# First block's inverse, edges and sums dealt out among its n_h products, and the first adjacency loads kept in text order: a two-layer graph network on one core

## The chip, the cores and the metric

The kernel runs on one core of a Trainium2 chip. The metric is the device time of one execution in microseconds (us); the time of a kernel is the median of its runs. Five engines work beside each other, each through its own instructions in order: TensorE (PE, matrix products; PEld is its weight load), VectorE (DVE), ScalarE (ACT), GpSimd (POOL) and SyncE (SP), which issues most of the transfers. They wait for each other through semaphores only.

## The reference, cut to what matters

`x` is 128 x 128 x 256 (batch, nodes, channels), `adj` 128 x 128 x 128 of zeros and ones, all in float32.

```python
h = relu(layernorm(x))
# layer 0, per batch element
c  = relu(bn1(conv1x1(h.T)));  c = bn2(conv17(c))          # along the nodes
x_conv = relu(c + h.T).T
s  = h @ w_se.T + b_se                                     # 3 columns
A  = exp(-dist(s, s)) * adj
x_nmp = A @ relu(h @ w_msg.T + b_msg)
gi = concat(x_conv, x_nmp) @ w_ih.T + b_ih
gh = h @ w_hh.T + b_hh
r, z = sigmoid(gi_r + gh_r), sigmoid(gi_z + gh_z)
n  = tanh(gi_n + r * gh_n)
x  = x + (1 - z) * n + z * h
# layer 1: five groups of the first 25 nodes, relu(layernorm(x)) again as input
for g in groups:
    N  = dinv * (adj_g + I) * dinv                         # dinv = deg ** -0.5
    o  = relu(N @ relu(N @ h_g @ W1[g] + b1[g]) @ W2[g] + b2[g])
    fused[idx_g] += softmax(fusion_w)[g] * o
x = x + fused
```

## The kernel before

The 128 batch elements go in 32 blocks of four. A front part (up to some 482 us) makes the normalised input `ht` of every block and stores it, and does the 17-wide convolution in the frequency domain: weight spectra, input spectra, products per frequency (`spectral`, lines 309 to 320), whose results lie in DRAM as `yd`. Then a main loop runs over the blocks and does the rest of layer 0; layer 1 goes in four parts (40, 40, 40 and 8 elements), the first from block 10 on, in the gaps of the main loop.

For block i the main part has these steps, each a function:

- `load(i)` (lines 458 to 473) issues on SP the loads of `ht`, of the adjacency `at`, of the frequency rows `ym` and of `yr` (four pieces of 32 rows).
- `gate_inputs(i, which)` (line 615) builds sums of quarter matrices, named `t` (lines 623 to 626, four operations of 128 x 256): `which` 2 from `ht`, 0 from `xc`, 1 from `xn`. They let a 2 x 2 block product be done with seven products in place of eight. In the kernel before those of `ht` and `xc` run on POOL, those of `xn` on DVE.
- `messages(i)` (lines 523 to 567) makes the messages `msg` and the three columns of `s` in seven products (line 535), combined on DVE (545, 546, 547, 552 to 555), ACT (548 copies `m5`) and POOL (549, 550), and ends with `lr`, the factors of the distance (561 to 566).
- `conv_out(i)` (lines 505 to 520) is the inverse of the frequency step: per half of the channels four products from `ym` (512) and one from `yr` (515), DVE adds `ht` (517), ACT takes the relu (518); the result is `xc`. It is a generator that stops after each half.
- `edge_terms(i)` transposes `lr` (573) into `lt` (copy on ACT, 575); `edges(i)` multiplies them (585), takes the exponential on ACT (588) and masks with `at` on DVE (590), giving `A_s[i]`.
- `x_nmp(i)` multiplies messages and edges (600) and copies out `xn` (603 on DVE, 605 on ACT).
- `gates(i, ...)` (line 631) does the gates in units of seven products (649), with copies on ACT (652, 660), sums on DVE (654, 657, 664, 667, 670) and on POOL (662, 668). Unit `nh` (gh_n) reads `ht` alone, `r` reads `ht`, `xc`, `xn`, `nn` reads `xc`, `xn`, and `z` all three. Sigmoid (684, 701) and tanh (694) run on ACT; 688, 693, 699, 702 and 703 are DVE's steps between. After each product the unit calls `between`.
- `back(i)` adds the result to `xt` (789), stores nodes 25 to 127 (`out`, 800) and the first 25 (`xf`, 802), and prepares layer 1's input (812 to 835). `degrees` makes the degree factors in steps (735 to 759), transposes (764) and stores them (767).
- `prepare(j)` (line 841) concerns pack j of layer 1: it loads the adjacency `nt` (846) and the factors `dck` (848, broadcast from the stored degrees) of pack j + 5, and for pack j + 2 adds the identity (852) and multiplies by `dck` (853). `nt` has eight buffers, `dck` three. Layer 1's first part calls it for j = -5 to -1 as it starts.

`beside_gates(i)` chains messages, inverse, edge terms, edges and x_nmp of block i with the back of block i - 2, one step for each `next`. In the main loop `gates(i, step, ...)` lets `step` advance block i + 1 between the products of block i. Block 0 has no block before it: its own steps run ahead of the loop until `A_s[0]` exists, and the rest of them after the sixth of its seven `nh` products (`sums_ahead`).

Where a region isn't scheduled by hand (the front is), the framework's planner orders every engine's instructions itself, so that text order isn't the order of the program: an instruction can be put earlier or later on its engine than the text has it. A buffer of a pool is given to the next tile once its last reader is placed, and that tile's first writer waits for it. PSUM has eight banks, handed on in the same way. SP issues transfers in order; an issue that has to wait holds up those behind it.

Of the kernel before, what the change touches and what calls it, by code (L numbers as in the profile page):

```python
# [75 lines left out]
def gnn_kernel(ctx: ExitStack, tc: tile.TileContext, io, out0: bass.AP, out1: bass.AP):  # L76
    nc = tc.nc
    x, adjT = io["x"], io["adjT"]
    B, N, D = x.shape
    C = D // P  # L80
# [24 lines left out]
    ident = cst.tile([P, P], F32)  # L105
# [248 lines left out]
    with front as es:  # L354
# [71 lines left out]
        begin = heads_begin(hk, xk, 3, 1)  # L426
        sums = gate_weights()
        amid = {p: lambda: next(begin, None) for p in range(16, NP_, 4) if p != 20}
# [29 lines left out]
    loaded, hts = {}, {}  # L458
# [45 lines left out]
    def conv_out(i):  # L504

        ht = hts[i]
        _, ym, yr = loaded[i]
        xc = wk.tile([P, C, T], F32, tag="xc", name="xc", bufs=2)
        for o in range(C):
            ps = bank()  # L510
            for b in range(BB):
                nc.tensor.matmul(ps[:, b * N:(b + 1) * N], ym[:, b, o * P:(o + 1) * P], idm,  # L512
                                 start=b == 0, stop=False)

            nc.tensor.matmul(ps.rearrange("p (b n) -> p b n", b=BB)[:, :, OUTW:], yr[:, o * P:(o + 1) * P], idr,  # L515
                             start=False, stop=True)
            nc.vector.scalar_tensor_tensor(xc[:, o, :], ps, sc2[:, o:o + 1], ht[:, o, :], op0=ALU.mult, op1=ALU.add)
            nc.scalar.activation(xc[:, o, :], xc[:, o, :], AF.Relu, bias=sh2[:, o:o + 1])
            yield
        xcs[i] = xc  # L520

    def messages(i):

# [91 lines left out]
    def gate_inputs(i, which=(0, 1, 2)):  # L615

        tt = ts.setdefault(i, {})
        for k in which:
            d, eng = ((xcs, nc.gpsimd), (xns, nc.vector), (hts, nc.gpsimd))[k]
            d = d[i]  # L620
            t = wk.tile([P, 4, H], F32, tag=f"t{k}", name=f"t{k}", bufs=1 + k // 2)
            b11, b12, b21, b22 = quarters(d)
            eng.tensor_tensor(t[:, 0], b12, b11, op=ALU.subtract)
            eng.tensor_tensor(t[:, 1], b22, t[:, 0], op=ALU.subtract)
            eng.tensor_tensor(t[:, 2], b22, b12, op=ALU.subtract)
            eng.tensor_tensor(t[:, 3], t[:, 1], b21, op=ALU.subtract)
            tt[k] = t

    def gates(i, between, nxt, ahead=None):

        ht, xc, tt = hts.pop(i), xcs.pop(i), ts[i]
        ins = [xc, None, ht]

        def small(name):
            return wk.tile([P, H], F32, tag=name, name=name, bufs=2)

        def unit(g, pairs, dst, order, hook=None, between=between):
            got = {}  # L640
            for j in order:
                ps = bank()[:, :H]
                for n, k in enumerate(pairs):
                    a11, a12, s1, a22 = (v[:, g] for v in gate_blocks(k))
                    s2, s3, s4 = (sw[k][:, g, m] for m in range(3))
                    b11, b12, b21, b22 = quarters(ins[k])
                    t1, t2, t3, t4 = (tt[k][:, m] for m in range(4))
                    w, d = ((a11, b11), (a12, b21), (s4, b22), (a22, t4), (s1, t1), (s2, t2), (s3, t3))[j - 1]
                    nc.tensor.matmul(ps, w, d, start=n == 0, stop=n == len(pairs) - 1)  # L649
                if j == 1:  # L650
                    got["m1"] = small("m1")
                    nc.scalar.copy(got["m1"], ps)
                elif j == 2:
                    nc.vector.tensor_tensor(dst[:, 0, :H], ps, got["m1"], op=ALU.add)
                elif j == 6:
                    got["u2"] = small("u2")
                    nc.vector.tensor_tensor(got["u2"], ps, got["m1"], op=ALU.add)
                elif j == 5:
                    got["m5"] = small("m5")
                    nc.scalar.copy(got["m5"], ps)  # L660
                    got["u4"] = small("u4")
                    nc.gpsimd.tensor_tensor(got["u4"], got["u2"], got["m5"], op=ALU.add)  # L662
                elif j == 3:
                    nc.vector.tensor_tensor(dst[:, 0, H:], ps, got["u4"], op=ALU.add)  # L664
                elif j == 7:
                    got["u3"] = small("u3")
                    nc.vector.tensor_tensor(got["u3"], ps, got["u2"], op=ALU.add)  # L667
                    nc.gpsimd.tensor_tensor(dst[:, 1, H:], got["u3"], got["m5"], op=ALU.add)
                else:
                    nc.vector.tensor_tensor(dst[:, 1, :H], got["u3"], ps, op=ALU.subtract)  # L670
                    if hook:
                        hook()
                between()

        o = wk.tile([P, C, T], F32, tag="o", name="o", bufs=2)
        r = o
        nh = wk.tile([P, C, T], F32, tag="z", name="nh", bufs=1)
        if ahead:

            unit(2, (2,), nh, (1, 2, 6, 5, 3, 7, 4), between=ahead)  # L680
        ins[1] = xns.pop(i)
        unit(0, (2, 0, 1), r, (1, 2, 6, 5, 3, 7, 4))
        for q in range(C):
            nc.scalar.activation(r[:, q, :], r[:, q, :], AF.Sigmoid, bias=brz[:, q:q + 1])
        if not ahead:
            unit(2, (2,), nh, (1, 2, 6, 5, 3, 7, 4))
        for q in range(C):
            nc.vector.scalar_tensor_tensor(r[:, q, :], nh[:, q, :], vec[:, V_HH + 4 + q:V_HH + 5 + q], r[:, q, :],
                                           op0=ALU.add, op1=ALU.mult)
        nn = wk.tile([P, C, T], F32, tag="nn", name="nn", bufs=1)  # L690
        unit(2, (0, 1), nn, (1, 2, 6, 5, 3, 7, 4))
        for q in range(C):
            nc.vector.tensor_add(nn[:, q, :], nn[:, q, :], r[:, q, :])  # L693
            nc.scalar.activation(nn[:, q, :], nn[:, q, :], AF.Tanh, bias=vec[:, V_IH + 4 + q:V_IH + 5 + q])  # L694
        z = wk.tile([P, C, T], F32, tag="z", name="z", bufs=1)
        unit(1, (2, 0, 1), z, (1, 6, 5, 7, 4, 2, 3), nxt)

        for q in range(C):
            nc.vector.tensor_sub(o[:, q, :], ht[:, q, :], nn[:, q, :])
        for q in range(C):  # L700
            nc.scalar.activation(z[:, q, :], z[:, q, :], AF.Sigmoid, bias=brz[:, 2 + q:3 + q])
            nc.vector.tensor_mul(o[:, q, :], o[:, q, :], z[:, q, :])
            nc.vector.tensor_add(o[:, q, :], o[:, q, :], nn[:, q, :])
        outs[i] = o
# [135 lines left out]
    def prepare(j):  # L840

        if 0 <= j + 5 < NPK:
            s, nb = GROUPS[PACKS[j + 5][1][0]][0], PACKS[j + 5][1][2]
            n = nb * s
            nt = l1.tile([P, P], F32, tag="nt", name="nt", bufs=8)
            nc.sync.dma_start(nt[:n, :n], io["adjN"][j + 5, :n, :n])
            dc = l1.tile([P, P], F32, tag="dck", name="dck", bufs=3)
            nc.sync.dma_start(dc[:n, :n], dvk[j + 5, :n].partition_broadcast(n))
            loads1[j + 5] = n, nt, dc
        if 0 <= j + 2 < NPK:  # L850
            n, nt, dc = loads1.pop(j + 2)
            nc.vector.tensor_add(nt[:n, :n], nt[:n, :n], ident[:n, :n])
            nc.vector.tensor_mul(nt[:n, :n], nt[:n, :n], dc[:n, :n])
            ready[j + 2] = nt

# [135 lines left out]
    def beside_gates(i):  # L991

        ends = back(i - 2, *back_loads(i - 2)) if i > 1 else iter(())
        if i < NBLK:
            parts = messages(i)
            next(parts)
            yield
            next(parts)
            next(ends, None)
            yield  # L1000
            inverse = conv_out(i)
            next(inverse)
            next(ends, None)
            yield
            edge_terms(i)
            next(ends, None)
            yield
            for _ in inverse:
                yield
            edges(i)  # L1010
            yield
            next(ends, None)
            yield
            yield
            yield from x_nmp(i)
        for _ in ends:
            yield
            if i == NBLK:
                yield
# [3 lines left out]
    degs = degrees(*degree_loads())  # L1023
    gate_inputs(0, (2,))
    begin = beside_gates(0)
    while 0 not in A_s:
        next(begin)
    gate_inputs(0, (0,))
    gate_inputs(1, (2,))
    held = [6]  # L1030

    def sums_ahead():

        held[0] -= 1
        if held[0] == 0:
            for _ in begin:
                pass
            gate_inputs(0, (1,))

    layer1s = []  # L1040
    for i in range(NBLK):
# [168 lines left out]
```

## Time and profile before

| | us |
|---|---|
| median of 4 runs | 1910.31 |
| the four runs | 1908.65, 1913.48, 1911.97, 1908.22 |
| the profiled execution | 1908.65 |
| its span, first to last instruction | 1906.8 |
| PE busy in the span | 1878.6 (99%) |
| DVE, ACT, POOL busy | 1343.0, 723.9, 667.4 |
| stage 500 to 520: PE, DVE busy | 18.97, 19.29 |
| stage 540 to 560: PE busy, mean granted clock | 16.96, 0.91 |
| stage 580 to 600: PE busy, mean granted clock | 19.96, 1.00 |

The page gives the busy time and the share of the span for each engine. A stage row (start:end) has the length of the stage, then busy time and instruction count of PE, PEld, DVE, ACT and POOL, then the clock granted to PE, the share of the DMA engines in use and GB/s. A timeline row has start, duration, engine, line, operation, what it writes and reads, shape and count; in brackets stands how long the engine was idle before it and what released it. A row of SPq is the issue of a transfer, not the transfer.

### The profile page before, as it was taken

How to read it: one execution, taken by the hardware profiler on the slowest of the kernel's cores; microseconds unless marked ns; L12 is line 12 of the kernel's file. 1: busy time of each engine (PE TensorE's matmuls, PEld its weight loads, DVE VectorE, ACT ScalarE, POOL GpSimd, SP SyncE). 2: the span in 40 equal slices, each digit the busy share in tenths (PEclk: the TensorE clock that was granted, in tenths of full speed). 3: DMA queues.
4: the chain of work that ended last, by engine and by line, in shares of the span. 5: the costliest groups of instructions: out<-in, count | busy, mean ns of one | idle time of the engine just before them, and what ended most of it. 6: DMA issues, size and time to landing. Idle time of an engine off the chain costs nothing.

```text
span 1906.8 us, 31441 instructions
## 1 busy us (share of the span) xinstructions
PE 1878.6 (99%) x10994; PEld 1643.4 (86%) x10994; DVE 1343.0 (70%) x3246; ACT 723.9 (38%) x1588; POOL 667.4 (35%) x747
## 2 busy tenths in 40 slices
PE   9999999999999999999999999999999999999998
PEld 7888889988788888888888888888888888888887
DVE  6674558754778787887666777878666688787643
ACT  5552124411333433343343343343343434334334
POOL 1113531265335445444312244544322244444200
PEclk9999999999999999999999999999999999999999
DMA  9976896289832332233244433233334434222135
GB/s 354 331 293 209 304 321 211 100 285 308 243 89 73 92 92 74 73 98 97 73 106 96 131 90 84 73 90 105 83 89 93 142 75 107 66 79 69 36 92 152
DMA packets 248877, 265.87 MB, mean 139 GB/s; under 512 B 106866, under 2 KB 223943, under 8 KB 244239
## 3 DMA queue, kind: packets, MB, share of 16 engines
q1 hardware_dynamic: 238751, 199.82, 37.5%
q10 hardware_dynamic: 9968, 64.04, 8.6%
q8 instruction: 88, 1.44, 0.3%
q14 instruction: 70, 0.57, 0.1%
HBM read 178.66 MB, written 85.14 MB: 138 GB/s over the span
## 4 chain that ended last, share of the span: by engine, by line
PE 91%; DMA 3%; DVE 3%; POOL 1%; issue 1%; ACT 0%; SPq 0%; POOLq 0%; DVEq 0%; ACTq 0%
PE bank L649 45%; PE bank L319 6%; PE bank L974 5%; PE bank L914 5%; PE bank L535 5%; PE bank L228 5%; PE bank L243 3%; PE bank L314 3%; PE bank L600 3%; PE bank L512 3%; PE bank L167 2%; DMA v<-vd 2%; PE bank L515 1%; PE bank L893 1%; PE bank L214 1%; PE bank L825 1%
## 5 line engine op out<-in xcount | busy, mean ns | idle before, releaser
L649 PE MATMUL bank<-t,sw 128*128 128x256 f32 x1152 | 291.3, 380 | 0.0
L662 POOL TENSOR_TENSOR u<-u,m 128x256 f32<-128x256 f32 x128 | 95.0, 742 | 485.3 <-ACT m L660 432.9
L649 PEld LDWEIGHTS bank<-t,sw 128*128 128x128 f32 x1152 | 215.4, 190 | 29.8 <-issue 2.3
L649 PE MATMUL bank<-t,wih 128*128 128x256 f32 x768 | 197.2, 379 | 0.0
L649 PEld LDWEIGHTS bank<-t,wih 128*128 128x128 f32 x768 | 143.4, 190 | 19.3 <-issue 0.5
L311 POOL TENSOR_TENSOR vs<-v 128x512 f32<-128x512 f32 x78 | 101.1, 1315 | 116.3 <-DMA v<-vd 67.1
L228 PE MATMUL bank<-wc,ht 128*128 128x256 f32 x512 | 118.9, 385 | 1.4 <-ACT ht L215 1.4
L649 PE MATMUL bank<-xc,wih 128*128 128x256 f32 x384 | 116.9, 386 | 0.7 <-DVE nh L664 0.2
L649 PE MATMUL bank<-t,whh 128*128 128x256 f32 x384 | 115.0, 381 | 2.3 <-DVE u L667 2.3
L558 ACT ACTIVATE msg<-msg 128x512 f32<-128x512 f32 x64 | 36.8, 621 | 210.7 <-DVE msg L554 210.7
L974 PE MATMUL bank<-w,hh 128*125 128x256 f32 (+9 forms) x480 | 113.8, 380 | 1.7 <-DVE hh L919 1.7
L649 PE MATMUL bank<-xn,wih 128*128 128x256 f32 x384 | 114.2, 379 | 0.0
L649 PE MATMUL bank<-ht,whh 128*128 128x256 f32 x384 | 110.0, 380 | 0.0
L228 PEld LDWEIGHTS bank<-wc,ht 128*128 128x128 f32 x512 | 96.3, 192 | 15.5 <-ACT ht L215 2.9
L914 PE MATMUL bank<-ax,w 128*128 128x500 f32 (+8 forms) x416 | 107.0, 396 | 0.3 <-DMA w<-in_w_dram 0.3
L309 DVE SCALAR_TENSOR_TENSOR s<-X 128x256 f32<-128x256 f32 x78 | 49.1, 632 | 82.0 <-PE bank L319 81.4
L198 POOL TENSOR_TENSOR rs<-ve,mhalf 128x4 f32<-128x4 f32 x32 | 32.8, 1026 | 205.0 <-DVE ve L196 205.0
L974 PEld LDWEIGHTS bank<-w,hh 128*125 128x125 f32 (+9 forms) x480 | 84.2, 177 | 20.3 <-DVE hh L919 2.6
L694 ACT ACTIVATE nn<-nn,vec 128x512 f32<-128x512 f32 x64 | 46.2, 722 | 135.8 <-DVE nn L693 135.8
L316 ACT COPY k<-bank 128x256 f32<-128x256 f32 x78 | 29.0, 373 | 175.6 <-DVE ys L320 70.7
L667 DVE TENSOR_TENSOR u<-bank,u 128x256 f32<-128x256 f32 x128 | 53.4, 417 | 57.7 <-PE bank L649 57.6
L314 PE MATMUL bank<-vs,X 128*128 128x256 f32 x312 | 81.6, 383 | 6.1 <-POOL vs L311 6.1
(207 smaller groups left out, 4519.8 us busy)
## 6 DMA issues: line engine op xcount, KB each, us to landing
v<-vd SPq DMA_DIRECT2D x80, 512.0 KB
vd<-sp ACTq DMA_DIRECT2D x8, 2560.0 KB
yd<-ys ACTq DMA_DIRECT2D x40, 512.0 KB
w<-in_w_dram SPq DMA_DIRECT2D x40, 512.0 KB
ln<-in_x_dram SPq DMA_DIRECT2D x32, 512.0 KB
htd<-ht ACTq DMA_DIRECT2D x32, 512.0 KB
ht<-htd SPq DMA_DIRECT2D x32, 512.0 KB
ym<-yd SPq DMA_DIRECT2D x32, 512.0 KB
```

Of the source, the lines that this page charges most:

```text
L228: nc.tensor.matmul(pv[:, bb, :], ht[:, c, b * N:(b + 1) * N], wc1[:, c, :], start=c == 0, stop=c == C - 1)
L243: nc.tensor.matmul(ps[:, bb * 2 * LW:(bb + 1) * 2 * LW], h1[:, 2 * h + bb, c * P:(c + 1) * P], fd, start=True, stop=True)
L311: nc.gpsimd.tensor_tensor(vs, vr, vi, op=ALU.add)
L314: nc.tensor.matmul(p1[:, :D], a[:, c], vs[:, c], start=c == 0, stop=c == C - 1)
L319: nc.tensor.matmul(ps[:, k * D:(k + 1) * D], u[:, c], w[:, c], start=c == 0, stop=c == C - 1)
L512: nc.tensor.matmul(ps[:, b * N:(b + 1) * N], ym[:, b, o * P:(o + 1) * P], idm, start=b == 0, stop=False)
L535: nc.tensor.matmul(ps[:, b, :], d[:, b * N:(b + 1) * N], w, start=True, stop=True)
L600: nc.tensor.matmul(ps[:, b * N:(b + 1) * N], msg[:, b, c * P:(c + 1) * P], e[:, b, :], start=True, stop=True)
L649: nc.tensor.matmul(ps, w, d, start=n == 0, stop=n == len(pairs) - 1)
L662: nc.gpsimd.tensor_tensor(got["u4"], got["u2"], got["m5"], op=ALU.add)
L914: nc.tensor.matmul(pv[:, q - q0, :], w1s[k5 + g][:, c, q * P:(q + 1) * P], xv[:, c], start=c == 0, stop=c == C - 1)
L974: nc.tensor.matmul(ps[:n1, :D], hh[:, q, at:at + n1], w2s[k5 + g][:, q, :], start=q == 0, stop=q == HID // P - 1)
```

## The change

Four edits. `conv_out` enters its result as it ends its last half, not one step later, and `beside_gates` skips a block's inverse if it was made ahead. The sums of `ht` of block 0 go from POOL to DVE. The steps of block 0 and the inverse of block 1 are called from a generator, `amid_first`, one portion after each of the seven `nh` products of block 0, where before most ran ahead of them and the rest after the sixth. In `prepare`, for j below 0, the two loads and the addition are passed through `tc.keep_in_program_order`, which keeps the instructions given to it in the order of the text.

```diff
@@ conv_out
             nc.scalar.activation(xc[:, o, :], xc[:, o, :], AF.Relu, bias=sh2[:, o:o + 1])
-            yield
-        xcs[i] = xc
+            if o == C - 1:
+                xcs[i] = xc
+            yield
@@ gate_inputs
-            d, eng = ((xcs, nc.gpsimd), (xns, nc.vector), (hts, nc.gpsimd))[k]
+            d, eng = ((xcs, nc.gpsimd), (xns, nc.vector), (hts, nc.gpsimd if i else nc.vector))[k]
@@ gates
-        ht, xc, tt = hts.pop(i), xcs.pop(i), ts[i]
-        ins = [xc, None, ht]
+        ht, tt = hts.pop(i), ts[i]
+        ins = [None, None, ht]
...
-        ins[1] = xns.pop(i)
+        ins[:2] = xcs.pop(i), xns.pop(i)
@@ prepare
-            nc.sync.dma_start(nt[:n, :n], io["adjN"][j + 5, :n, :n])
+            pin = tc.keep_in_program_order if j < 0 else lambda ins: ins
+            pin(nc.sync.dma_start(nt[:n, :n], io["adjN"][j + 5, :n, :n]))
             dc = l1.tile([P, P], F32, tag="dck", name="dck", bufs=3)
-            nc.sync.dma_start(dc[:n, :n], dvk[j + 5, :n].partition_broadcast(n))
+            pin(nc.sync.dma_start(dc[:n, :n], dvk[j + 5, :n].partition_broadcast(n)))
             loads1[j + 5] = n, nt, dc
         if 0 <= j + 2 < NPK:
             n, nt, dc = loads1.pop(j + 2)
-            nc.vector.tensor_add(nt[:n, :n], nt[:n, :n], ident[:n, :n])
+            pin = tc.keep_in_program_order if j < 0 else lambda ins: ins
+            pin(nc.vector.tensor_add(nt[:n, :n], nt[:n, :n], ident[:n, :n]))
             nc.vector.tensor_mul(nt[:n, :n], nt[:n, :n], dc[:n, :n])
@@ beside_gates
-            inverse = conv_out(i)
-            next(inverse)
+            inverse = iter(()) if i in xcs else conv_out(i)
+            next(inverse, None)
@@ ahead of the main loop
     begin = beside_gates(0)
-    while 0 not in A_s:
+    for _ in range(3):
         next(begin)
-    gate_inputs(0, (0,))
-    gate_inputs(1, (2,))
-    held = [6]
+    second = conv_out(1)
+
+    def amid_first():
+
+        next(begin)
+        yield
+        next(begin)
+        gate_inputs(0, (0,))
+        yield
+        while 0 not in A_s:
+            next(begin)
+        yield
+        next(second)
+        yield
+        gate_inputs(1, (2,))
+        yield
+        for _ in begin:
+            pass
+        gate_inputs(0, (1,))
+        yield
+        for _ in second:
+            pass
+        yield
+
+    amid = amid_first()
 
     def sums_ahead():
-
-        held[0] -= 1
-        if held[0] == 0:
-            for _ in begin:
-                pass
-            gate_inputs(0, (1,))
+        next(amid)
```

## The prediction

> **What bounds the kernel now.** I read the page first. The profiled execution took 1908.65 us around a span of 1906.8, and the median of the four runs is 1910.31, 1.66 above it.
>
> ```profile
> span 1906.8 us, 31441 instructions
> PE 1878.6 (99%) x10994; PEld 1643.4 (86%) x10994; DVE 1343.0 (70%) x3246; ACT 723.9 (38%) x1588; POOL 667.4 (35%) x747
> ```
>
> TensorE idles 28.2 us in all, so a reordering can only win idle time or lost clock. The built orders of both programs hold the same matrix products and differ only between 481 and 570 us, but for four small VectorE operations put off to some 930 us. The timeline of PE there shows every stall of size, each with its releaser in brackets.
>
> ```profile
> 484.16 0.71 PE L535 MATMUL bank<-swm,t 128*128 128x130 f32 x4 [1.40 <-POOL t L624]
> 490.22 0.41 PE L573 MATMUL bank<-ident,lr 128*128 128x128 f32 x2 [2.23 <-DVE lr L566]
> 503.68 0.68 PE L535 MATMUL bank<-wms,t 128*128 128x130 f32 x4 [1.01 <-DVE nh L670]
> ...
> 551.27 0.70 PE L649 MATMUL bank<-t,whh 128*128 128x256 f32 x2 [2.34 <-DVE u L667]
> ...
> 553.09 0.56 PE L585 MATMUL bank<-lt 5*128 5x128 f32 x4 [0.70 <-ACT m L652]
> ...
> 557.44 0.59 PE L649 MATMUL bank<-xc,wih 128*128 128x256 f32 x2
> ```
>
> Behind the fourth stands VectorE, in order and held by an adjacency factor (dck) that SP issued behind a store:
>
> ```profile
> 549.89 0.29 DVE L853 TENSOR_TENSOR nt<-nt,dck 125x125 f32<-125x125 f32 x1 [2.38 <-DMA dck<-dvk]
> 550.59 0.29 DVE L853 TENSOR_TENSOR nt<-nt,dck 125x125 f32<-125x125 f32 x1 [0.41 <-DMA dck<-dvk]
> ```
> ```profile
> 541.50 0.64 SPq L800 DMA_DIRECT2D out_dram<-xt  x1
> 543.37 0.52 SPq L802 DMA_DIRECT2D xf<-xl  x1
> 544.27 1.55 SPq L848 DMA_DIRECT2D dck<-dvk  x3
> 548.35 0.36 SPq L1058 DMA_DIRECT2D xt<-in_xT_dram  x1
> ```
> ```profile
> 554.00:557.00 3.00, 3.00 (x9) 2.52 (x8) 1.48 (x5) 2.78 (x7) 0.89 (x2) 0.50 0.52 173
> ```
>
> The last row (stages; the 0.50 is the granted clock) shows that the pause also cost half the clock; from 553.96 to 557.37 by the clock record, 1.7 us of work. One block later the same products, from the first t,sw to xc,wih, take 594.19 - 590.48 = 3.71 us; here 557.44 - 548.34 = 9.10. This place costs 5.4 us, the first three stalls 4.64; all gone would be 10.0 us, or 0.5%.
>
> **The change, part by part.** I step the changed program's order with the durations of these rows; lines are those of the kernel before. PE advances 0.22 us for a 128x128 or 128x130 product, 0.43 for a 256-column one.
>
> *Sums of hts on VectorE.* In the VectorE rows around 502 such an operation starts every 0.33 us; POOL took 0.73 each. VectorE was free at 482.59 (L545 started there), so the third sum ends at 482.59 + 0.66 + 0.42 = 483.67, not 484.11. L545 follows at 483.93, and the chain through m5 and POOL u4 to lr comes 0.55 earlier: transposes at 489.67 instead of 490.22, with one n_h product (0.43) done inside the wait. PE is 0.98 ahead.
>
> *Block 1's inverse among the products.* Its first product comes 0.24 + 0.43 + 0.89 + 0.43 + 0.43 + 0.44 + 0.43 = 3.29 us after the transposes, at 492.96. It needs block 1's ym. Before, that was first read at 506.79, so nothing shows there; but SP's second dgc issue, at 494.28, was released by that ym. New wait 1.3; the yr pieces land around 495.2, as the product that needs them comes. The first attention sum starts at 496.5 instead of 495.01, with 1.32 us of inverse more behind it: 0.2 behind. The 0.98 is spent. If ym landed with the ht one place before it (491.2, when POOL was released), 1.3 would stay won; it can't be worse than 495.2.
>
> *The 1.01 wait goes*: L670 is done at 503.8, and PE, with both inverse halves (2.64) done, gets to its bank at 504.3. The first r product with second sums starts at 505.75 against 504.20: 1.1 ahead.
>
> *What is queued behind the new waits.* VectorE's L735 starts only when dga lands (497.67), and both L517 of block 1 (0.66 each) now lie behind it and ahead of block 1's lr, which ends at 510.45, not 509.53. PE waits 0.95 there: 0.3 ahead. ScalarE's second xn copy goes behind L518 of block 1, to 501.1; PE needs it at 503.1, covered; uncovered it is 0.6. Waits of 0.1 to 0.15 at 509.59 and 519.74 have cover now, so at the degree transposes PE is **0.7 ahead** (524.35 against 525.08).
>
> *SP.* The ym and four yr of block 3 (0.39 and about 1.8 us of issue) go ahead of block 1's xt, ae and the first w. Their inverse is over by 500, so SP doesn't wait as it did until 513.54; xt is first read some 30 us later, and w after 900. I cost this at nothing; without that cover it is 2.2.
>
> *Loads in text order.* SP now issues dck0, nt1, dck1, nt2, dck2 after the degree stores. But the pinned additions of packs 0 and 1 stay in text order too: they and their multiplications go to some 930 us. So two of three dck buffers stay occupied, and the built program puts the dck of packs 2 to 8 all at one address. Each load must wait for the multiplication before it, and VectorE, in order, waits for each load.
>
> Step by step: the first addition on VectorE is now pack 2's, whose nt is the fourth load from dck0 on; the loads so placed before landed 5.9 us after issue (issued 530.25; the trace keeps each transfer's landing), so VectorE idles 1.5 and the second L789 ends at 539.0. The store goes out 2.5 us earlier than before and lands 6.85 later (548.35 - 541.50), at 545.85. The dck of pack 3, issued 540.3 behind it, takes the 5.6 us of 544.27 to 549.89: 545.9. VectorE idles from 542.6 to there, but PE needs its next bank (L517) at 547.3 and gets it. The dck of pack 4 is issued at 546.3 behind xt; bounds are 2.7 (nt, 527.04 to 529.78, nothing ahead) and 5.6. I take 3.5, since only a load, no store, is ahead, as with the dck of 550.21 (3.6 by its landing time): 549.8. L670 follows at 550.1; PE waits for its bank from 548.3 to 550.5 (2.2). The block's statistics free the next bank at 552.25 (1.3), L654 at 552.6 (0.25). The dck of pack 5 (550.2 + 3.5 = 553.7) holds the second L517 to 554.65: 1.6 more. The t,sw product of 554.25 comes at 554.7. Before, 5.48 us passed from 548.77 to it with 1.30 us of products in them, 4.2 lost; now 6.35 us pass from 548.35 with 0.87, 5.5 lost. Of the 1.3 more, the head start pays 0.85 (the 0.7, and 0.1 of small waits before 548), and PE is 0.45 late. The dck of pack 7, issued about 562.8 behind the xa stores, holds VectorE some 2 us at 564.5; banks last until about 572, covered. The four late operations (4 x 0.3 to 0.8) meet VectorE 13.07 busy of 25 us (stage from 925); uncovered, up to 2.
>
> The Trainium skill speaks against the change twice, and the sum needs neither. "DMA: Bandwidth & Descriptors", section "Queues, rings and completion order": a DMA's completion mark lands only after every earlier write of that DMA engine. The 5.6 us behind the store agree, and by the rule pack 3's factor can't land before the store's 545.85, while without it 540.3 + 2.7 = 543.0 were possible; PE notices neither. "TensorE: Matmul & The Clock Gate", Part 1: activity is judged in free-running windows of about 3.4 us, a mostly idle one halving the clock. The record's 3.41 us agrees; by the rule 5.5 us lost of 6.35 make one or two slow windows where the row alone says one as before: 1.7 us more in the second case.
>
> Sum: t,sw 0.45 late; from there to xc,wih it took 3.19 us at half clock, until 557.37, so that 0.52 us of it now fall behind that moment and take half: 0.45 - 0.26. I take **+0.2 us** on the span, that is no change: 1910.31 + 0.2 = **1910.5**. With each factor load 0.8 faster or slower (two links count) it is 1.6 either way, and one slow window less or more: 1907.2 to 1913.8.
>
> **Rivals.** A measurement of this kernel tells 0.2% (3.8 us) from no change; I count that as the bound.
>
> *The factors come in time (faster).* VectorE has two pairs of nt operations less by 541 and reaches L664 at 542.4, not 546.43. If packs 4 and 5 load in 2.7 or less and nothing holds xt, the place at 548 to 557 goes: -0.7 - 5.4 = -6.1, **1904.2**. Against it: one address, and SP can't issue pack 4's dck before the store has landed.
>
> *The chain stalls harder (slower).* One mechanism: the single dck buffer. If packs 4 and 5 each take the 5.6 of the row behind a store, L670 and then L517 slip by 2.1 each, 4.2, and the longer pause costs the 1.7 of half clock once more: 0.2 + 5.9 = +6.1, **1916.4**. It decides from 5.3 us a link (2 x 1.8 = 3.6 over the forecast). For it: xt, half a megabyte, is right ahead of pack 4's. Against: 3.6 for the load behind the xt of 548.35.
>
> *It does what it says early, without the ym wait*: -1.3 more, 1909.2, inside the forecast. That it doesn't do what it says can be ruled out in part: the built order has loads and additions in text order, but not all of them early.
>
> **How the numbers follow.** Forecast 0.50, factors in time 0.18, harder stalls 0.32. Faster by over 0.2%: 0.18; within: 0.50; slower: 0.32. The range 1904.0 to 1917.0 takes in both rivals' times and leaves out the further part of each, some 0.08 and 0.12; the forecast alone is 1907.2 to 1913.8.
>
> **What would show it.** PE released by DMA ym at the first inverse product of block 1 (about 1.3 us); no L670 wait near 503; a wait on lr near 510; the second L789 near 539; L853-like multiplications released by DMA dck at about 546, 550 and 553.5, and PE behind L670 and L517 there; a clock of 0.50 for one window or two. I am wrong if VectorE has no such waits, or if PE stalls where I have cover (572, 930).

## The result, and the profile after

The changed kernel takes 1913.9 us (median of 53 runs, 1908.97 to 1922.63); the kernel before, measured beside it, 1909.58 (78 runs, 1903.92 to 1918.65). The ratio is 1.0021 with a 95% interval of 1.0015 to 1.0027: 4.0 us more, 2.9 to 5.2.

Lines of the changed kernel are a few higher than those of the kernel before: L650 is its L649, L671 its L670, L857 its L853, L851 its L848. First the page, the span and TensorE's row:

```profile
span 1912.1 us, 31432 instructions
PE 1882.2 (98%) x10994; PEld 1645.8 (86%) x10994; DVE 1342.1 (70%) x3250; ACT 723.6 (38%) x1588; POOL 665.2 (35%) x743
```

The span is 5.3 longer. Not all of it is the change's: the stage begins 1.74 later, since the clock record shows half clock from 205.20 to 212.02 in this execution (205.80 to 209.22 before), where the two programs are the same. To set a time of this profile beside one of before, 1.74 has to be taken off. TensorE's timeline, the rows with an idle time ahead (in brackets, with what ended it):

```profile
485.56 0.69 PE L536 MATMUL bank<-swm,t 128*128 128x130 f32 x4 [1.05 <-DVE t L625]
...
491.62 0.41 PE L574 MATMUL bank<-ident,lr 128*128 128x128 f32 x2 [1.84 <-DVE lr L567]
...
495.83 1.13 PE L512 MATMUL bank<-idm,ym 128*128 128x128 f32 x8 [0.55 <-DMA ym<-yd]
...
550.93 0.70 PE L650 MATMUL bank<-t,sw 128*128 128x256 f32 x2 [2.70 <-DVE xc L517]
551.47 0.69 PE L650 MATMUL bank<-t,whh 128*128 128x256 f32 x2
553.38 0.80 PE L586 MATMUL bank<-lt 5*128 5x128 f32 x4 [1.22 <-DVE o L671]
...
557.95 1.22 PE L650 MATMUL bank<-t,sw 128*128 128x256 f32 x2 [1.24 <-DVE xc L517]
...
931.30 0.70 PE L650 MATMUL bank<-xc,wih 128*128 128x256 f32 x2 [0.42 <-DVE nh L665]
```

The early waits are smaller (1.05 for 1.40, 1.84 for 2.23), the 1.01 near 503 is gone, there is a new one on ym, and at 550 us stand three waits where before had 2.34 and 0.70. Behind the three stands VectorE; its timeline there:

```profile
545.38 0.42 DVE L665 TENSOR_TENSOR o<-bank,u 128x256 f32<-128x256 f32 x1 [1.12 <-POOL u L663]
548.66 0.29 DVE L857 TENSOR_TENSOR nt<-nt,dck 125x125 f32<-125x125 f32 x1 [2.86 <-DMA dck<-dvk]
549.92 0.29 DVE L856 TENSOR_TENSOR nt<-nt,ident 125x125 f32<-125x125 f32 x1 [0.97 <-DMA nt<-in_adjN_dram]
550.13 0.74 DVE L517 SCALAR_TENSOR_TENSOR xc<-bank,bn,ht 128x512 f32<-128x512 f32 x1
...
552.61 0.29 DVE L857 TENSOR_TENSOR nt<-nt,dck 125x125 f32<-125x125 f32 x1 [1.21 <-DMA dck<-dvk]
552.82 0.41 DVE L671 TENSOR_TENSOR o<-u,bank 128x256 f32<-128x256 f32 x1
...
556.94 0.29 DVE L857 TENSOR_TENSOR nt<-nt,dck 125x125 f32<-125x125 f32 x1 [1.96 <-DMA dck<-dvk]
557.15 0.74 DVE L517 SCALAR_TENSOR_TENSOR xc<-bank,bn,ht 128x512 f32<-128x512 f32 x1
```

Each of the three VectorE operations that TensorE waited for (L517, L671, L517) starts 0.2 us after an nt operation that had waited for a load: the first after the addition of 549.92 (an nt load), behind the multiplication of 548.66, the others after a multiplication (a dck load). This is the chain on one dck buffer. SP issued its first load behind the first block's store:

```profile
539.98 0.64 SPq L801 DMA_DIRECT2D out_dram<-xt  x1
540.72 0.61 SPq L803 DMA_DIRECT2D xf<-xl  x1
541.43 1.01 SPq L851 DMA_DIRECT2D dck<-dvk  x1
542.50 0.82 SPq L849 DMA_DIRECT2D nt<-in_adjN_dram  x2
```

By the trace's landing times the store was complete at 546.93, xf at 547.30, pack 3's dck at 548.64 (7.2 after issue), the two nt at 549.90 and 550.46.

To set kernels side by side I cut each trace at the same products of TensorE, counted from the start: the beginning of the stage (478.69 in before), the end of the dealt-out products (523.35), the beginning and the end of the pause's place (541.94 and 564.41), and two later ones (870.34, 963.74). In brackets is the half-clock time inside.

| us | to 523.35 | to 541.94 | place, to 564.41 | to 870.34 | to 963.74 |
|---|---|---|---|---|---|
| before | 44.67 (0) | 18.58 | 22.47 (3.41) | 305.94 | 93.40 |
| after | 43.07 (0) | 18.25 | 27.62 (10.24) | 305.91 | 94.04 |

In these two profiles the change wins 1.60 + 0.33 + 0.03 and loses 5.15 in the place and 0.64 near 931: 3.8 us net, which the interval of the medians holds. The first two terms are not the usual gain. In a second profile of the changed kernel (below) the first stretch took 44.21, and in a second profile of the kernel before the second stretch took 18.25 too (the first took 46.18 there, with 6.83 at half clock).

### The profile page after: what moved, and what is told of

The parts are those of the page before. It is cut to its first block, busy times and chain, and to the rows that moved or that the text cites. A ratio compares the mean times of both kernels' runs of the same rounds, so it can differ in the third digit from the quotient of the medians.

```text
span 1912.1 us, 31432 instructions
## 1 busy us (share of the span) xinstructions
PE 1882.2 (98%) x10994; PEld 1645.8 (86%) x10994; DVE 1342.1 (70%) x3250; ACT 723.6 (38%) x1588; POOL 665.2 (35%) x743
## 3 DMA queue, kind: packets, MB, share of 16 engines
q8 instruction: 88, 1.44, 0.3%
## 4 chain that ended last, share of the span: by engine, by line
PE 90%; DMA 5%; DVE 3%; POOL 1%; issue 1%; ACT 0%; SPq 0%; ACTq 0%; POOLq 0%; DVEq 0%
PE bank L650 45%; PE bank L319 5%; PE bank L978 5%; PE bank L918 5%; PE bank L536 5%; PE bank L228 4%; PE bank L601 3%; PE bank L243 3%; PE bank L512 3%; PE bank L314 3%; DMA v<-vd 2%; PE bank L167 2%; PE bank L515 1%; PE bank L897 1%; PE bank L214 1%; PE bank L826 1%
## 5 line engine op out<-in xcount | busy, mean ns | idle before, releaser
L650 PE MATMUL bank<-t,sw 128*128 128x256 f32 x1152 | 291.5, 380 | 3.9 <-DVE xc L517 3.9
L650 PEld LDWEIGHTS bank<-t,sw 128*128 128x128 f32 x1152 | 215.3, 190 | 34.7 <-DVE xc L517 5.4
L650 PE MATMUL bank<-t,wih 128*128 128x256 f32 x768 | 197.2, 379 | 0.0
L650 PEld LDWEIGHTS bank<-t,wih 128*128 128x128 f32 x768 | 143.4, 190 | 19.3 <-DVE u L668 0.5
L650 PE MATMUL bank<-xc,wih 128*128 128x256 f32 x384 | 117.7, 388 | 1.0 <-DVE nh L665 0.4
L650 PE MATMUL bank<-t,whh 128*128 128x256 f32 x384 | 115.2, 382 | 0.0
L650 PE MATMUL bank<-xn,wih 128*128 128x256 f32 x384 | 114.7, 380 | 0.0
L650 PE MATMUL bank<-ht,whh 128*128 128x256 f32 x384 | 110.1, 380 | 0.0
L650 PEld LDWEIGHTS bank<-xc,wih 128*128 128x128 f32 x384 | 71.1, 191 | 19.8 <-DVE nh L665 11.0
```

## The experiments

**Which edit.** Four kernels each take a part of the change alone or undo one.

*The pins alone* (the new `prepare` in the kernel before, nothing dealt out):

```diff
+            pin = tc.keep_in_program_order if j < 0 else lambda ins: ins
+            pin(nc.sync.dma_start(nt[:n, :n], io["adjN"][j + 5, :n, :n]))
...
+            pin(nc.vector.tensor_add(nt[:n, :n], nt[:n, :n], ident[:n, :n]))
```

> Only the new prepare in the kernel before; nothing is dealt out. Theory (late additions of packs 0 and 1 leave one dck buffer, a chain): VectorE waits for dck three times between 548 and 558 us, TensorE's pause there grows by 3 to 5 us, and nothing is won early: 3 to 6 us slower than before, ratio 1.0016 to 1.0031, as slow as the changed kernel or slower. Rival (the dealing-out costs, by the new wait on ym and VectorE's new order): the early stage is the old one, so 1.000.

Measured 1912.09 us, ratio 1.0015 (1.000 to 1.003). VectorE waits for dck here too, but its timeline shows another order:

```profile
548.70 0.74 DVE L517 SCALAR_TENSOR_TENSOR xc<-bank,bn,ht 128x512 f32<-128x512 f32 x1
551.87 0.29 DVE L856 TENSOR_TENSOR nt<-nt,dck 125x125 f32<-125x125 f32 x1 [2.43 <-DMA dck<-dvk]
...
557.13 0.74 DVE L517 SCALAR_TENSOR_TENSOR xc<-bank,bn,ht 128x512 f32<-128x512 f32 x1
557.79 0.41 DVE L657 TENSOR_TENSOR u<-bank,m 128x256 f32<-128x256 f32 x1
559.98 0.29 DVE L856 TENSOR_TENSOR nt<-nt,dck 125x125 f32<-125x125 f32 x1 [1.78 <-DMA dck<-dvk]
```

Both L517 stand ahead of the multiplications of packs 3 and 5, which in the changed kernel stand ahead of them. TensorE waits 2.44 and 0.22 in all, the place takes 23.64 (6.83 at half clock), and of the 3 to 5 us more that I expected there nothing is seen beside the 23.33 that a second profile of before shows (below). *The dealing-out alone*:

```diff
-            pin = tc.keep_in_program_order if j < 0 else lambda ins: ins
+            pin = lambda ins: ins
```

> The changed kernel without the pins. Theory: the early stage is 1.6 us ahead at the degree transposes, three dck buffers rotate, and the pause at 548 us is the old one (4 to 5 us of idle time, the factors of packs 4 to 7 behind the store): 1 to 3 us faster than before, ratio 0.9984 to 0.9995. Rival (the dealing-out costs): 1.0015 to 1.003.

Measured 1906.96, ratio 0.9989 (0.9977 to 1.0001). TensorE's waits in its place sum to 3.2 where the changed kernel has 5.3:

```profile
549.95 0.70 PE L650 MATMUL bank<-t,sw 128*128 128x256 f32 x2 [1.22 <-DVE xc L517]
552.73 0.49 PE L586 MATMUL bank<-lt 5*128 5x128 f32 x4 [1.47 <-DVE o L671]
553.71 0.61 PE L586 MATMUL bank<-lt 5*128 5x128 f32 x4 [0.49 <-ACT m L653]
```

Its place takes 22.90. So in these profiles neither edit alone makes the 27.62: the pins make the chain of loads, and it is in the order that the build arrives at with the dealing-out that L517 waits behind it. The medians can't carry this: both intervals reach 1.000, and that of the pins alone also holds the changed kernel's 1.0021. It rests on the place in one profile of each, and on VectorE's order, which is the build's. The rival that the dealing-out by itself is the loss falls: without the pins the interval (up to 1.0001) lies below the changed kernel's.

*Four dck buffers* (and seven nt, to make room):

```diff
-            nt = l1.tile([P, P], F32, tag="nt", name="nt", bufs=8)
+            nt = l1.tile([P, P], F32, tag="nt", name="nt", bufs=7)
-            dc = l1.tile([P, P], F32, tag="dck", name="dck", bufs=3)
+            dc = l1.tile([P, P], F32, tag="dck", name="dck", bufs=4)
```

> The changed kernel with four dck buffers in place of three, and seven nt in place of eight to make room; additions and loads stay pinned. Theory (the chain on one buffer): with two buffers left pack 3's factor is loaded ahead of the store and those of packs 4 and 5 side by side behind it, so that TensorE loses 4 to 5 us there as before, not 9: 3 to 6 us faster than the changed kernel, ratio to before 0.9985 to 1.0. Rival (it is where the pinned loads stand on SP's queue, not the buffers): stays at 1.002.

Measured 1907.01, ratio 0.9996 (0.9981 to 1.0011). *Loads pinned, additions not*:

```diff
-            pin(nc.vector.tensor_add(nt[:n, :n], nt[:n, :n], ident[:n, :n]))
+            nc.vector.tensor_add(nt[:n, :n], nt[:n, :n], ident[:n, :n])
```

> The changed kernel with the loads pinned and the additions of packs 0 and 1 not. Theory (what hurts is that the pinned additions keep two dck buffers): three buffers rotate again, the factor of pack 3 is issued ahead of the store, those of packs 4 to 6 side by side behind it, and TensorE loses 4 to 6 us at 548 us as before: 1 to 3 us faster than before, ratio 0.9985 to 0.9995. Rival (the loads' place on SP's queue hurts): 1.0015 to 1.003, as the changed kernel.

Measured 1907.86, ratio 0.9994 (0.9979 to 1.0009). With a buffer freed in either way, and the loads still pinned, the upper ends (1.0011, 1.0009) lie below the changed kernel's interval: it is not where the loads stand on SP's queue, but the buffers that the late additions hold. (Unpinning the additions also changes VectorE's order; the fourth buffer leaves the additions late.) Neither shows the 1 to 3 us that I expected to win on before; the place takes 24.18 and 24.39, somewhat over the 22.47 and 23.33 of before.

**Is it VectorE's waiting?** *All additions late*: the addition of every pack pinned, so that the multiplications and the loads that need their buffers go late as well:

```diff
-            pin = tc.keep_in_program_order if j < 0 else lambda ins: ins
+            pin = tc.keep_in_program_order
             pin(nc.vector.tensor_add(nt[:n, :n], nt[:n, :n], ident[:n, :n]))
```

> The changed kernel with the addition of every pack pinned, so that no nt work is left on VectorE before some 920 us. Theory (VectorE held in order by dck is all of the pause at 548 us): no wait on dck there, TensorE's pause gone with its half clock, 1.6 + 5.4 = 7 us faster than before, ratio 0.9963, as long as the 16 operations more (about 0.3 us each, 5 us) find cover after 920; if they do not, up to 5 us come back, 0.999. Rival (the pause has another cause, such as the new state's own store and loads): 1.000 to 1.002.

Measured 1896.39 us, ratio 0.9935 (0.9915 to 0.9955): 12.4 us faster than before, and faster than the changed kernel. Its place (the row gives length, then busy time and count of PE, PEld, DVE, ACT, POOL, then the granted clock):

```profile
537.53:554.33 16.80, 16.80 (x103) 14.96 (x102) 13.34 (x36) 8.91 (x19) 4.65 (x6) 1.00 0.49 126
```

TensorE never pauses there and keeps its whole clock. Stretch by stretch, from the stage's beginning to 963.74, this kernel is 6.5 us ahead of before (43.64, 18.25, 16.80, 305.84, 94.01), near the 7 expected. The rest of the 12 is not shown to be the edit's: this execution had no half clock ahead of its last 4 us, where that of before had 3.41 at 205.80, in code that the edit does not touch, and its runs were few (6). The expected 0.9963 lies outside the interval; two kernels below whose place is as short or nearly so, with 12 runs each, measured 0.9961 and 0.9960.

*No factors*: the dck loads left out and each nt multiplied by the identity, which leaves out the degree scaling of layer 1 but keeps VectorE's operations where they are.

```diff
-            dc = l1.tile([P, P], F32, tag="dck", name="dck", bufs=3)
-            pin(nc.sync.dma_start(dc[:n, :n], dvk[j + 5, :n].partition_broadcast(n)))
-            loads1[j + 5] = n, nt, dc
+            loads1[j + 5] = n, nt, ident
```

> The changed kernel without the dck loads: each nt is multiplied by the identity instead, so the degree scaling of layer 1 is left out. VectorE keeps the same additions and multiplications between 525 and 560 us, and nothing there waits for a factor. Theory (waiting for dck is the loss, not VectorE's 0.3 us operations): TensorE's pause at 548 us is gone or under 1.5 us, ratio 0.996 to 0.998. Rival (the operations themselves keep L517 and L670 back, being ahead of them in order): 0.9995 to 1.002.

Measured 1901.11, ratio 0.9961 (0.9947 to 0.9976). TensorE's one wait left there is

```profile
546.70 0.70 PE L650 MATMUL bank<-xc,wih 128*128 128x256 f32 x2 [0.42 <-DVE nh L665]
```

and the place takes 17.86, as against 16.80. So VectorE's operations cost some 1 us of the place, and waiting for factors, with the loads that stand behind them on SP's queue and the half clock that came with it, is the rest: 27.62 - 17.86 = 9.8 us in the changed kernel.

*All late, nothing dealt out* (the kernel before with this `prepare`):

> The kernel before with the loads and the addition of every pack pinned, nothing dealt out. Theory: the pause at 548 us is gone here too, 5 to 7 us, and the difference to the run with dealing-out is what dealing-out is worth, 1.0 to 1.5 us in the early stage: ratio 0.996 to 0.9975. Rival (only both together win, since the early stage decides what meets the store): 0.999 to 1.001.

Measured 1899.94, ratio 0.9961 (0.9947 to 0.9975); place 17.08. Stretch by stretch it is 1.09, 0.28, 0.08 and 0.03 behind the run with dealing-out, 1.48 in this pair of profiles, as expected. But the first stretch varies from profile to profile: in the eight with the dealt-out order of the changed kernel and no half clock there it took 43.07 to 44.37, in the two with the old order 44.67 and 44.73. So dealing out is worth 0.3 to 1.7 us there, and the medians can't tell it (the intervals overlap).

*A further step from there*: two pieces swapped in `amid_first` of the kernel with all additions late.

```diff
-        next(second)
-        yield
         gate_inputs(1, (2,))
         yield
+        next(second)
+        yield
```

> The run with all additions late, with the first half of block 1's inverse and that block's sums of hts swapped among the pieces dealt out, so that one product of 0.43 us more stands ahead of the inverse's wait on ym. Theory: the wait shrinks from 1.23 to about 0.8, all else stays: 0.4 us faster than that run, ratio to before 0.992 to 0.996. Rival (sums placed earlier hold POOL or VectorE ahead of the attention's own operations): up to 1 us slower than that run, 0.994 to 0.997.

Measured 1898.77, ratio 0.9960 (0.9946 to 0.9975). The ym wait was 0.95, a yr wait of 0.21 and one of 0.32 on lr came in, and the stretch to 523.35 took 44.34 for 43.64. No gain is shown, and no loss either: without the swap the wait ahead of that product was 0.55 to 1.84 in nine profiles and the stretch up to 44.37, so that one profile can't show a step of 0.4, and by the medians it can't be told from either neighbour.

**Why 7.2 us for a factor?** *The out store on ScalarE's queue*, then *both stores*:

```diff
-        nc.sync.dma_start(out0[i], xv[:, :, :, NN:])
+        (nc.scalar if i == 0 else nc.sync).dma_start(out0[i], xv[:, :, :, NN:])
```

> The changed kernel with the first block's out store issued by ScalarE, so that the factor of pack 3 is not behind it on SP's queue; the single buffer and its chain stay. Theory of the landing (a load's completion is held by the store's packets, whichever queue issued them): the factor still takes 6 to 7.5 us and lands after the store; 0 to 1 us from the changed kernel. Rival (the queue's order holds it): it takes 2.7 to 4 us, VectorE's first wait of 2.86 shrinks below 0.5, TensorE's first stall of 2.70 goes with it, and the kernel is 2 to 4 us faster than the changed one, about 1.000 of before.

Measured 1915.14, ratio 1.0032 (1.0015 to 1.0049). The factor took 7.8, but xf was still ahead of it on SP's queue. The time can't be told from the changed kernel's (1.0015 to 1.0027), but the place can: in this build pack 3's multiplication stands ahead of lr in VectorE's order, waits 5.40, and TensorE waits 4.36 for lr; half clock rose to 13.65 and the place to 31.71. The same edit for xf as well:

> The changed kernel with both stores of the first block (out and xf) issued by ScalarE, so that no store is ahead of pack 3's factor on SP's queue. Theory (the stores' packets hold the load's completion, whichever queue issued them): the factor, issued within 1.5 us of the stores, still takes 6 to 8 us and lands after them. Rival (the order on SP's queue holds it): 2.7 to 4 us, landing ahead of the out store.

One run, 1920.5 us. ScalarE's and SP's issues overlap (out at 542.65, xf at 543.36, dck at 543.56), and no store is ahead of the factor on its own queue:

```profile
550.25 0.29 DVE L857 TENSOR_TENSOR nt<-nt,dck 125x125 f32<-125x125 f32 x1 [4.16 <-DMA dck<-dvk]
```

The factor landed at 550.23, 6.7 after issue; out landed at 549.90, xf at 550.70. In this run it is not the order on SP's queue that holds it. That it lands after out fits the theory, that it lands 0.5 ahead of xf does not quite; whether the stores' completion or only their load on the DMA engines holds it stays open.

**Is the half clock chance?** Both kernels unaltered, for second profiles:

> The changed kernel unaltered, for a second profile. Theory (the clock is judged on a grid of 3.41 us whose place differs from run to run, so the same pause makes two or three slow windows): the same waits to 0.2 us (2.70, 1.22 and 1.24 on TensorE; pack 3's factor 7.0 to 7.4 us), but 6.8 or 10.2 us at half clock at 550 us and a stage loss from 541 to 572 us that differs by up to 1.7 us from the first profile. Rival (the three windows belong to this kernel): 10.2 us again.

> The kernel before unaltered, for a second profile. Theory: the same waits (2.34 and 0.70), 3.4 or 6.8 us at half clock. Rival (one window belongs to this kernel): 3.4 us again.

One run each, 1917.19 and 1906.12 us. The changed kernel's place took 26.99 with 10.24 us at half clock again, though its waits were 1.62, 1.63, 0.25 and 1.18 and the factor took 6.50; the kernel before took 23.33 with 6.83, with one wait of 2.75. So the number of slow windows changed from profile to profile in the kernel before, as the theory had it. For the changed kernel 10.24 again is what the rival named, and the theory allowed it too: two profiles don't decide it. What failed in both is that the waits would be the same. The clock's windows, read off the clock record of the first profile (PE's busy time is the first after the length, its granted clock third from the end), show how the slow time went on:

```profile
546.53:549.95 3.42, 1.70 (x12) 1.27 (x10) 0.32 (x2) 0.03 (x1) 0.00 (x0) 1.00 0.55 174
549.95:553.36 3.41, 1.23 (x4) 0.61 (x5) 2.20 (x8) 1.02 (x3) 0.73 (x1) 1.00 0.25 78
553.36:556.77 3.41, 3.15 (x10) 1.93 (x10) 1.59 (x7) 1.45 (x3) 0.56 (x1) 0.50 0.57 156
556.77:560.19 3.42, 2.24 (x6) 2.00 (x7) 1.73 (x5) 2.25 (x3) 0.72 (x1) 0.50 0.23 73
560.19:563.60 3.41, 3.41 (x10) 2.73 (x9) 3.41 (x8) 1.17 (x6) 1.16 (x1) 0.50 0.12 35
563.60:567.01 3.41, 3.41 (x21) 3.10 (x21) 2.44 (x9) 0.59 (x2) 0.00 (x0) 1.00 0.58 128
```

and in the kernel before:

```profile
547.13:550.55 3.42, 1.80 (x12) 1.35 (x11) 0.67 (x2) 1.40 (x3) 0.00 (x0) 1.00 0.69 121
550.55:553.96 3.41, 1.99 (x12) 1.26 (x12) 3.00 (x9) 1.49 (x3) 1.29 (x2) 1.00 0.53 149
553.96:557.37 3.41, 3.41 (x10) 2.83 (x9) 1.89 (x6) 3.05 (x7) 1.26 (x2) 0.50 0.47 156
```

At half clock, a window with TensorE idle in part (3.15, 2.24) was followed by another slow one, a wholly busy window (3.41) by the full clock. This is so in the place in every profile with half clock there, but not everywhere: at 205.80 in the kernel before a window with 3.17 busy was followed by the full clock, and at 488.62 in its second profile one with 3.41 by another slow one. Before, the pause was over and one busy window ended it. The changed kernel's third wait, 1.24 at 557, falls inside the slow time, in the window with 2.24 busy after which the clock stayed half; that it prolonged the slow time is read from these rows and was not tried by itself.

## Why the prediction was right, and where it was not

The forecast (+0.2 us) was 3.8 short, inside its range. The range held because it takes in the rivals: 1913.9 lies just past the forecast's own 1907.2 to 1913.8, and 4.0 us is slower by the bound of 0.2% that the prediction set, an outcome that it gave 0.32 and not 0.50. By its own steps:

*Early.* In the clock of before (1.74 taken off): the first product with the third sum 483.82 (predicted 483.7), lr's transposes 489.88 (489.67), attention sums 496.48 (496.5), r product 505.74 (505.75). The new wait on ym came, at 0.55 instead of 1.3, and the 1.01 of L670 went. The 0.95 on lr near 510 did not come: L567 ended at 509.43, not 510.45. At the degree transposes TensorE was 1.6 ahead, not 0.7. But this profile was lucky. In the eight others with the same early order TensorE waited 0.78 to 1.84 ahead of the first inverse product of block 1 (1.35 in the changed kernel's second profile), three had a wait of 0.13 to 0.48 on lr, and in the seven of them without half clock there the transposes came 0.3 to 1.0 before those of the kernel before, counted from the stage's beginning. The 1.3 and the 0.7 were about right. For the 0.7 that was partly luck: its written terms, 1.1 - 0.95 and two waits of 0.1 to 0.15, add up to 0.35 to 0.45.

*The chain.* The mechanism was right: one dck buffer, VectorE in order, waits at packs 3, 4 and 5, with TensorE behind L517, L671, L517. The links of packs 4 and 5 took 3.54 and 3.99 for the 3.5 taken. The step that failed is the first link, pack 3's. "The dck of pack 3, issued 540.3 behind it, takes the 5.6 us" and "PE needs its next bank (L517) at 547.3 and gets it" are its words. The load took 7.2 (6.5 in the second profile), and I overlooked that the nt of pack 4, loaded right behind it, is added ahead of L517: 0.97 more. L517 started at 548.39 in before's clock, and TensorE lost 2.70 that I had covered. The row I took, 544.27 to 549.89, was issued nearly 3 us after its store; here it was 1.45. That alone does not explain the 7.2: with the dealing-out alone a factor issued 1.44 after the store took 5.7. Why the first link took so long stays open.

*The clock.* I took one slow window, gave two as the other case; it was three, in both profiles. The place's stage row for the changed kernel

```profile
541.74:569.37 27.63, 22.30 (x102) 18.11 (x101) 15.49 (x48) 8.98 (x19) 4.63 (x6) 0.81 0.41 103
```

and for the kernel before

```profile
541.94:564.41 22.47, 19.43 (x103) 16.33 (x102) 15.85 (x51) 8.91 (x19) 5.16 (x7) 0.92 0.51 115
```

stand against 16.80 of the same products without a pause: 27.63 - 22.30 = 5.33 of idle time and 22.30 - 16.80 = 5.50 of longer work; before, 3.04 and 2.63. So the 5.15 lost are 2.29 of waiting and 2.87 of longer work. The clock record gives most of the latter: half of the busy time of the slow windows is (3.15 + 2.24 + 3.41) / 2 = 4.40, and 3.41 / 2 = 1.71 before, a difference of 2.69. The other 1.1 and 0.9 of longer work it does not tell. I had priced the clock as a single term after the pause, and not asked what a wait costs that falls inside the slow time. "TensorE: Matmul & The Clock Gate", Part 1, of the Trainium skill states that a busy window of about 3.4 us opens the clock; the rows above agree, with 3.41 of 3.41 busy where it opened and 3.15 where it did not, while the 3.41 at 488.62 in the second profile of before did not open it. The prediction's "mostly idle" is not the measure here: a window with 1.99 of 3.41 busy was followed by half clock, one with 1.70 was not.

*The cover at 930.* "The four late operations ... meet VectorE 13.07 busy of 25 us", costed at nothing, was wrong by 0.64, and a stall there is one of the signs of being wrong that the prediction named: that stretch took 94.00 to 94.04 in every profile with pinned additions that I cut there, and 93.38 to 93.40 in those without (both profiles of before, dealing-out alone, loads pinned alone). The row at 931.30 shows 0.42 of it. It goes with the pinned additions; that it is these four operations was not tried. The cover at 572 held.

*The rivals.* "The factors come in time" did not happen, but its price was about right: the kernel with all additions late wins 5.67 in the place where I had said 5.4. "The chain stalls harder" needs 5.3 for the links of packs 4 and 5; they did not take that. The loss came by the first link and the clock instead.

## What to carry to other kernels

Pinning one instruction late holds every buffer that its chain has yet to free: ask how many are left for the next loads, and what stands in order behind the operations that wait for those; two edits that apart left the place near its old length (23.64 and 22.90) met there (27.62). Work that nobody needs for 350 us is best moved whole, its loads too, away from a place where the engine in order feeds the bound one; moving part of it made the place longer by 5.15 us, moving all of it shorter by 5.67. And where the bound engine's clock falls with its idle time, waits close together can cost more than their sum: here 5.33 us of idle time came with 5.50 us of longer work.

## What the runs showed of the hardware

The entry to half clock does not follow the busy share of a single window: in the place, windows with 0.86 (before, second profile), 1.23, 1.69 (dealing-out alone) and 1.99 us of TensorE's 3.41 busy were followed by half clock, windows with 1.70, 1.80 and 1.97 (dealing-out alone) were not. The ends of products are modelled, so part of it may be the record's.

Half clock also came and went ahead of the stage, between 39 and 240 us and once at 435, in executions of programs whose TensorE, VectorE and SP orders are the same up to there. With none to 17 us of it, the stage began anywhere from 473.42 to 485.14; not all of that is the clock's, since the three executions with none began up to 2.7 apart. A difference of a few us between two spans says nothing here until the stretch is named in which it arose.

A factor of 61 KB took 5.3 to 7.8 us to land when it was issued within 1.5 us of one of the first block's stores (ten profiles: 6.5 to 7.8 in the changed kernel and the two with moved stores, 5.3 to 6.5 in the others), on the stores' queue or on another, and 2.7 to 4.1 in the links of the changed kernel's chain after that. One of 6.0 (issued at 533.35 in the run with both stores moved, with the half megabyte of ht 0.55 behind it) had no store of the block beside it, so other transfers can do the same. "DMA: Bandwidth & Descriptors", section "Queues, rings and completion order", of the Trainium skill says that a completion waits for the earlier writes of its DMA engine across queues; the run with both stores moved agrees in that the change of queue did not help, but can't tell it from mere load on the same engines.
